# A four-layer graph network on one core: score rows through DRAM in place of transposes, layer 0 divided as it leaves PSUM, and the end graphs' norms in halves

## The chip, the core and the metric

The kernel runs on one core of one Trainium2 chip. Times are device microseconds (us) of one execution. A kernel is run several times and its median is given; one more execution is recorded by the hardware profiler, and everything said of single instructions comes from that one.

## What is computed

The input is 32 graphs of N = 512 nodes with D = 256 features each, and an integer adjacency matrix of 512 x 512 for each graph. Four layers follow one another; each adds its result to its input and normalizes the sum over the features.

```python
# layer 0: four heads of 64, one kind of edge in these data
h = einsum('bnd,hde->bhne', x, W)
weight = leaky_relu(e_src[i] + e_dst[j], 0.01), closed where adj == 0
out = relu(softmax(weight) @ h + bias) + h
x = layernorm(x + (layernorm of out over each head) * gamma + beta)
# layer 1: one head, scores relu(f_src[i] + f_dst[j])
x = layernorm(x + elu(softmax(scores) @ (x @ W)))
# layer 2: a transformer block, 8 heads of 32, edges made symmetric
x1 = layernorm(x + attention(x) @ Wo + bo) * g1 + b1
t  = layernorm(x1 + relu(x1 @ W1 + c1) @ W2 + c2) * g2 + b2      # 256 -> 1024 -> 256
x  = layernorm(x + t)
# layer 3: one head, scores leaky_relu(f_i + f_j, 0.2)
x = layernorm(x + softmax(scores) @ (x @ W))
```

In layers 0, 1 and 3 a score is a function of a sum of one number for the node and one for its neighbour. The kernel takes the exponential of each part once (`ex`), and the unnormalized weight of a pair is the larger of two products of such numbers; so a tile of weights needs one of the parts as a row that lies the same on all 128 partitions (a **score row**, `gb`), and the other as a column.

## The kernel before

**Tiles.** A graph's 512 nodes are R = 4 blocks of 128 partitions; its features lie along the free dimension. All products are in float32. Layers 0, 1 and 3 are products of the 512 x 512 weights (`pt`, four tiles of 128 x 512 per head) with the projected features; layer 2 has scores `s`, their exponentials `pr`, context `cp`, the projection `wop`, and the feed-forward products `f1p` and `f2p`.

**Order.** Each graph is a Python generator that yields before each piece of TensorE work. `heapq.merge` takes the piece with the smallest due place, PERIOD x graph + PLACES[layer][piece] (lines 27 to 46), so that at any time layers 0 and 1 of a later graph, the attention of the one before it and the feed-forward and layer 3 of an earlier one are interleaved. TensorE executes in the order so written. The instructions of VectorE (DVE in the profile), ScalarE (ACT), GpSimd (POOL) and of the transfers (SP) are placed by a scheduler; each of these queues then runs strictly in its order, and an instruction that waits holds back all behind it. `keep_busy` (line 118) puts filler products, 128 x 512 in bf16, ahead of some pieces of the first two and the last two graphs, by the table BUSY (lines 47 to 55). All products have line 112 in the profile and are told apart by their tiles.

**Score rows.** `along` (lines 357 to 367) makes one score row of 512 from a column tile: four TensorE transposes of a column that is broadcast over 128, into one PSUM bank (`gp`), and one ACT copy of 128 x 512 to SBUF (`gb`). Layer 0 has four such rows (one a head), layers 1 and 3 one each. `kept` (line 424, `pt`) is the VectorE instruction that makes a tile of weights from row, column and edges.

**Layer 0** (lines 428 to 515). Products h0p of the inputs; `hv` holds the four heads' values, each with a column of its scale behind it (lines 448 and 453). For each block j, four `pt0`, then eight products `o0` and four `den0` of 32 columns each, four at a time side by side in the array. `den` sums the weights, `o0` holds the unnormalized output, with features on the partitions. Three ACT copies (`back`, L481) take them out of PSUM, twelve transposes (`backp`) turn them back, two reciprocals (L494) of the turned `den` give the divisor, and L501 divides while it applies relu. Then follow x + beta (L509), the addition of h (L510), the norm over each head (lines 306 to 319), gamma (L512), the residual (L513) and the layer's norm.

**Norms.** `layernorm` (lines 284 to 304) takes all four rows at once: four pairs of bn_stats and bn_aggr on VectorE (L290, L291), Ln and Exp on ACT (L282, L283), one small VectorE instruction (L293, `rs`) and four ACT instructions of 128 x 256 (L297), which write the normalized rows.

**Around it.** `transposed` (lines 326 to 338) turns a layer's input: eight transposes (xt1p, xt2p, ytp, xt3p) and two ACT copies (L337). Layer 1 is at lines 532 to 554: h1p, the score row gb1, four `pt1`, the products o1 (in the profile `o<-h,pt`), for each a reciprocal (L547) and two ACT passes (L548, L549), and for each pair of rows two VectorE instructions (L550, L552). In layer 2 the transfers qk (L584) spread the parts of q and k over partitions, L623 to L628 divide by `den`, L653 closes edges and L680 adds up weights. The feed-forward ends with L737 (residual), a norm, L739 and L740 and another norm; layer 3 is at lines 745 to 774, and the finished graph is stored by one transfer (L840). The inputs come by the transfers xt (L779), x (L784), adjt and adj (L372).

Of the kernel before, what the change touches and what calls it, by code (L numbers as in the profile page):

```python
# [28 lines left out]
    "edges": [-3978, -1720, -957, -79],  # L29
    "x": [5375],  # L30
    "mask": [14366, 15324, 18155, 20933],
    "layer 0": [
        -33568, -33515, -33424, -32942, 5301, 7043, 7043, 7043, 8766, 10194, 11091, 11128,
        11993, 11993, 14391,
    ],
    "layer 1": [15460, 15460, 15555, 15555, 15555, 15555, 16382, 17321, 17344, 17344, 17355, 17355],
    "qkv": [18153, 18153, 22255, 22255, 23139, 24065, 25534, 25534, 25534, 25534, 25534],
    "attention": [
        -5960, -4506, -4506, -3927, 26460, 26497, 26497, 26593, 26886, 27435, 27446, 27462,
        28434, 28434, 28779, 29106, 29409, 30200, 31616, 32371, 34290, 34290,  # L40
    ],
    "projection": [34382, 34412, 34412, 34412, 34443],
    "feed forward": [
        36011, 36047, 37566, 38431, 38431, 38519, 38519, 38646, 38646, 38732, 38732, 39499,
        39499, 39646, 39646, 40873, 41200, 41449, 41464,
    ],
    "layer 3": [44919, 44919, 44969, 44969, 44969, 44969, 45682, 48065, 48065, 48065, 48422, 48422],
}
BUSY = {
    ("layer 0", 9): {0: 16, 1: 6},  # L50
    ("layer 1", 1): {0: 72, 1: 40},
    ("layer 1", 8): {0: 4},
    ("layer 3", 1): {-2: 42, -1: 45},
# [27 lines left out]
def fast_path(ctx: ExitStack, tc: tile.TileContext, a: dict, out: bass.AP, bad: bass.AP):  # L81
# [8 lines left out]
    nc = tc.nc  # L90
# [12 lines left out]
    ND = R * (H + 2)  # L103
    NL = 6
    NV = R * (NL + H) + 2 * K
# [157 lines left out]
    ps = ctx.enter_context(tc.tile_pool(name="ps", bufs=2, space=bass.MemoryType.PSUM))  # L263
    stage = ["a"]
# [13 lines left out]
    def all_rows(v):  # L278
        return v.unsqueeze(1).to_broadcast([P, R, D])
# [5 lines left out]
    def layernorm(y, e, mv):  # L285

        st = buf([P, R, 6], "bn", "bn", 2)
        rs = buf([P, 2, R], "rs", "rs", 2)
        for r in range(R):
            nc.vector.bn_stats(st[:, r, :], y[:, r, :])  # L290
            nc.vector.bn_aggr(mv[:, r, :], st[:, r, :])  # L291
        inverse_root(rs[:, 0, :], mv[:, :, 1], e)
        nc.vector.scalar_tensor_tensor(  # L293
            rs[:, 1, :], mv[:, :, 0], -1.0, rs[:, 0, :], op0=ALU.mult, op1=ALU.mult
        )
        for r in range(R):
            nc.scalar.activation(  # L297
                y[:, r, :],
                y[:, r, :],
                AF.Identity,  # L300
                bias=rs[:, 1, r : r + 1],
                scale=rs[:, 0, r : r + 1],
            )

    def head_layernorm(y, e, var):

        G = R * H
        yg = y.rearrange("p r (g d) -> p (r g) d", g=H)
        st = buf([P, 2, G], "lnh", "st", 2)
# [3 lines left out]
        for i in range(2):  # L313
            g = slice(i * G // 2, (i + 1) * G // 2)
            sq = part("sq").rearrange("p (g d) -> p g d", d=HO)
            nc.scalar.activation(sq, yg[:, g, :], AF.Square, scale=HO**-0.5)
            nc.vector.tensor_reduce(var[:, g], sq, axis=X, op=ALU.add)
# [39 lines left out]
    def along(cols, name):  # L357

        yield
        p = bank("gp")  # L360
        for r in range(R):
            product(nc.tensor.transpose,
                    p[:, r * P : (r + 1) * P], cols[:, r, :].to_broadcast([P, P]), ident
            )
        g = part(name)
        nc.scalar.copy(g, p)  # L366
        return g
# [60 lines left out]
    def layer0(x, xt, at, rd, mv, var):  # L428
# [25 lines left out]
        gbs = []  # L454
        for hh in range(H):
            gbs.append((yield from along(ex[:, 0, hh, :].unsqueeze(2), "gb0")))
        den, *ops = (bank(name) for name in ("den0", "o0", "o0"))
        for j in range(R):
            pt = [kept("pt0", gbs[hh], at[:, j, :], ex[:, 1, hh, j : j + 1]) for hh in range(H)]
            yield  # L460
            for hh in range(H):
                for e in range(0, HO, DH):
                    product(nc.tensor.matmul,
                        ops[hh // 2][hh % 2 * HO + e : hh % 2 * HO + e + DH, :],
                        hv[:, j, hh, e : e + DH],
                        pt[hh],
                        start=j == 0,
                        stop=j == R - 1,
                    )
            for hh in range(H):  # L470
                product(nc.tensor.matmul,
                    den[hh * DH : (hh + 1) * DH, :],
                    hv[:, j, hh, HC - DH :],
# [3 lines left out]
                )  # L477
        back = []
        for i, o in enumerate((den, *ops)):
            t = part("back")  # L480
            nc.scalar.copy(t, o)  # L481
            back.append(t)
        y = sb.tile([P, R, D], F32, tag="y", name="y0", bufs=3)
        for i in range(1 + H // 2):
# [6 lines left out]
            if i == 0:  # L491
                rdh = rd.rearrange("p (i r h) -> p i r h", i=H // 2, r=R)
                for i in range(H // 2):
                    nc.vector.reciprocal(  # L494
                        rdh[:, i],
                        p.rearrange("p (r h e) -> p r h e", r=R, h=H)[
                            :, :, 2 * i : 2 * i + 2, DH - 1
                        ],
                    )
                continue  # L500
# [1010 lines left out]
```

## Time and profile before

| | |
|---|---|
| runs | 3490.72, 3491.74, 3490.98 us; median 3490.98 |
| profiled execution | 3491.36 us, of which the span from first to last instruction is 3489.5 |
| mean granted TensorE clock | 0.996 of full |
| instructions | 51983, of these 18579 products and transposes on TensorE |
| HBM | 106.57 MB read, 16.78 MB written; DMA engines busy 32% of the span |

TensorE's queue runs nearly without a gap. The slices of the profile (fortieths of the span) tell where it does not: in the first two and the last one. The first graphs and the last ones have no neighbours to fill the waits of their chains. Between them the picture repeats with every graph. A line of a timeline gives start, length, engine, line, operation, output and inputs, the tile's size and how many instructions it joins; in brackets stands how long the engine had been idle and what ended that. A group of the profile gives total busy time, the mean length of one in ns, and the idle time before. Lengths of TensorE's instructions overlap; the distance of two starts tells what one costs in the queue.

### The profile page before, as it was taken

To read this page: it belongs to the slowest core of one execution; us is meant where nothing else is said; L and a number is where in the kernel's file an instruction comes from. 1 tells how busy PE (TensorE), PEld (TensorE's weight loads), DVE (VectorE), ACT (ScalarE), POOL (GpSimd) and SP (SyncE) were. 2 spreads that over 40 slices of the span, in tenths; PEclk is the share of its full clock that TensorE was granted. 3 is DMA by queue.
4 is the path that set the end of the run, shared out by engine and by line. 5 is a ranking of instruction groups with operands and counts; after the bars stand their busy time and mean duration, and the time that the engine had idled before them with its cause. 6 is when DMAs were issued, how large, how long until landed. Compare 5 with 4: busy or idle time off the path is not lost.

```text
span 3489.5 us, 51983 instructions
## 1 busy us (share of the span) xinstructions
PE 3436.7 (98%) x18579; PEld 2383.9 (68%) x18579; DVE 2889.2 (83%) x5178; ACT 2222.6 (64%) x5729; POOL 81.7 (2%) x171
## 2 busy tenths in 40 slices
PE   7899999999999999999999999999999999999997
PEld 4466767776767776767776767776767776767765
DVE  5778888888888888888888889888889888889863
ACT  3556667666667666667666667666667666666653
POOL 0000000000000000000000000000000000000000
PEclk9999999999999999999999999999999999999999
DMA  4434232334232333232333232334232333232220
GB/s 132 85 76 91 61 85 59 81 79 91 61 85 59 81 79 91 61 85 60 80 79 91 62 84 61 79 79 91 62 84 61 79 79 91 63 84 55 54 55 13
DMA packets 164040, 261.04 MB, mean 75 GB/s; under 512 B 20416, under 2 KB 56384, under 8 KB 163776
## 3 DMA queue, kind: packets, MB, share of 16 engines
q1 hardware_dynamic: 163776, 257.65, 32.0%
q8 instruction: 150, 2.46, 0.3%
q14 instruction: 114, 0.93, 0.1%
HBM read 106.57 MB, written 16.78 MB: 35 GB/s over the span
## 4 chain that ended last, share of the span: by engine, by line
PE 94%; DVE 3%; ACT 1%; issue 1%; DMA 1%; SPq 0%; POOL 0%; ACTq 0%; DVEq 0%; POOLq 0%
PE o L112 20%; PE f2p L112 13%; PE f1p L112 13%; PE s L112 8%; PE qkp L112 6%; PE cp L112 6%; PE den L112 5%; PE h3p L112 3%; PE h1p L112 3%; PE wop L112 3%; PE vp L112 3%; PE h0p L112 3%; PE gp L112 2%; PE backp L112 1%; PE xt3p L112 1%
## 5 line engine op out<-in xcount | busy, mean ns | idle before, releaser
L653 DVE TENSOR_TENSOR pr<-pr,a 128x1024 f32<-128x1024 f32 x384 | 455.5, 1221 | 184.8 <-ACT pr L650 184.8
L424 DVE SCALAR_TENSOR_TENSOR pt<-gb,ex,at 128x512 f32<-128x512 f32 x768 | 538.2, 746 | 33.5 <-ACT gb L366 25.8
L650 ACT ACTIVATE pr<-s 128x512 f32<-128x512 f32 x1024 | 545.3, 617 | 3.0 <-PE s L112 3.0
L112 PE MATMUL f2p<-wf,ft 128*128 128x256 f32 x2048 | 484.8, 380 | 5.5 <-ACT ft L723 5.2
L112 PE MATMUL f1p<-yt,wf 128*128 128x256 f32 x2048 | 483.9, 379 | 0.0
L112 PE MATMUL o<-h,pt 128*128 128x257 f32 x2048 | 475.3, 382 | 2.7 <-DVE pt L424 2.7
L112 PEld LDWEIGHTS o<-h,pt 128*128 128x128 f32 x2048 | 385.6, 190 | 97.5 <-issue 41.8
L680 DVE TENSOR_TENSOR pr<-pr 128x1024 f32<-128x1024 f32 x384 | 447.3, 1213 | 2.8 <-PE cp L112 2.8
L112 PEld LDWEIGHTS f2p<-wf,ft 128*128 128x128 f32 x2048 | 384.0, 190 | 62.9 <-ACT ft L723 9.8
L112 PEld LDWEIGHTS f1p<-yt,wf 128*128 128x128 f32 x2048 | 389.1, 190 | 54.4 <-DVE lo L577 0.5
L297 ACT ACTIVATE y<-y,rs 128x256 f32<-128x256 f32 x768 | 398.1, 593 | 17.0 <-DVE rs L293 17.0
L112 PE MATMUL s<-qk 128*128 128x512 f32 x1024 | 376.5, 469 | 4.6 <-DMA qk<-lo 3.7
L723 ACT ACTIVATE ft<-f1p,cols 128x256 f32<-128x256 f32 x512 | 217.0, 469 | 236.1 <-PE f1p L112 235.3
L290 DVE BATCH_NORM_STATS2 bn<-y 128x6 f32<-128x256 f32 x768 | 300.0, 413 | 5.6
L112 PE MATMUL o<-pt,hv 128*32 128x512 f32 x2048 | 285.0, 602 | 4.7 <-DVE pt L424 4.7
L282 ACT ACTIVATE rs<-mvs,eps1e-05_70 128x4 f32<-128x4 f32 x192 | 57.6, 300 | 325.6 <-DVE mvs L291 321.7
L112 PE MATMUL qkp<-xt,wqkv 128*128 128x512 f32 x512 | 240.5, 603 | 0.0
L112 PE MATMUL cp<-pr,v 128*32 128x512 f32 x2048 | 234.2, 595 | 1.4 <-DVE pr L653 1.4
L112 PEld LDWEIGHTS s<-qk 128*128 128x128 f32 x1024 | 189.0, 192 | 55.5 <-issue 27.6
L112 PEld LDWEIGHTS o<-pt,hv 128*32 128x32 f32 x2048 | 72.7, 109 | 176.5 <-issue 87.4
L576 ACT ACTIVATE hi<-qkp,cols 128x512 fp32r<-128x512 f32 x128 | 88.4, 691 | 164.1 <-PE qkp L112 164.1
L769 DVE RECIPROCAL rd<-o 128x1 f32<-128x1 f32 x128 | 21.6, 168 | 177.5 <-PE o L112 177.3
(140 smaller groups left out, 4949.6 us busy)
## 6 DMA issues: line engine op xcount, KB each, us to landing
qk<-hi SPq DMA_DIRECT2D x512, 128.0 KB, 3.4
qk<-lo SPq DMA_DIRECT2D x512, 128.0 KB, 3.5
adjt<-in_adjt SPq DMA_DIRECT2D x64, 512.0 KB, 3.9
adj<-in_adj SPq DMA_DIRECT2D x64, 512.0 KB, 4.8
xt<-in_xt SPq DMA_DIRECT2D x32, 512.0 KB, 3.8
x<-in_x SPq DMA_DIRECT2D x32, 512.0 KB, 5.2
out<-y SPq DMA_DIRECT2D x32, 512.0 KB, 4.6
wf<-in_w1t SPq DMA_DIRECT2D x1, 1024.0 KB, 9.1
```

Source lines behind the costliest of these rows:

```text
L112: latest[0] = what(*args, **kwargs).ins.name
L282: nc.scalar.activation(out, variance, AF.Ln, bias=eps[e])
L290: nc.vector.bn_stats(st[:, r, :], y[:, r, :])
L297: nc.scalar.activation(y[:, r, :], y[:, r, :], AF.Identity, bias=rs[:, 1, r : r + 1], scale=rs[:, 0, r : r + 1],)
L424: nc.vector.scalar_tensor_tensor(t, g, f, edges, op0=ALU.max, op1=ALU.mult)
L576: nc.scalar.activation(hi, p, AF.Identity, bias=bias)
L650: nc.scalar.activation(t[:, i, :], s, AF.Exp, scale=QSCALE)
L653: nc.vector.tensor_mul(t, t, edges)
L680: nc.vector.tensor_add(t, t, u)
L723: nc.scalar.activation(ft[:, f, :], p[:, f, :], AF.Relu, bias=bf1[:, ff + f : ff + f + 1])
L769: nc.vector.reciprocal(rd[:, r : r + 1], p[:, D : D + 1])
```

## The change

For graphs 1 to 30, called the inner ones, `along` now gives all rows of a layer by one transpose of the columns (16 for layer 0, 4 for layers 1 and 3), one ACT copy of that many partitions by 128, one transfer (a write) into a tile in DRAM, and one transfer (a read) for each row of 512, which reads it from DRAM to all 128 partitions. The first and the last graph, the end graphs, make their rows as before.

In layer 0, `den` is no longer turned back. Its stationary operand is now the scale column broadcast to 32, so that its bank holds the divisor on the same partitions as the outputs; the order of the output's partitions is changed to fit. ACT takes the logarithm of `den` and the exponential of its negative (`inv`), with two sums for the range check; VectorE multiplies the two output banks by `inv` as they leave PSUM; eight transposes follow, and the last step takes relu and adds h in one instruction. The piece count of layer 0 goes from 15 to 11.

In the end graphs the norms of layers 0, 1, 3 and of the feed-forward go in halves of two blocks, and the output is stored in halves. The tiles that hold the values for the range check change size, one of them gets a fourth buffer. The table of due places is new in all layers, and the fillers are fewer: 186 instead of 237 are executed (the new entry for piece 13 of layer 0 is never reached, since the layer has 11). TensorE has 17770 instructions instead of 18579: 630 fewer gp transposes, 128 fewer backp, 51 fewer fillers.

The tables of due places are left out below, as are the lines that pass the graph's number on.

```diff
 BUSY = {
-    ("layer 0", 9): {0: 16, 1: 6},
-    ("layer 1", 1): {0: 72, 1: 40},
+    ("layer 0", 9): {0: 12, 1: 6},
+    ("layer 0", 13): {0: 10},
+    ("layer 1", 1): {0: 48, 1: 34},
     ("layer 1", 8): {0: 4},
-    ("layer 3", 1): {-2: 42, -1: 45},
+    ("layer 3", 1): {-2: 40, -1: 30},
     ("projection", 1): {-1: 8},
     ("layer 3", 8): {-1: 4},
 }
...
-    ND = R * (H + 2)
+    ND = R * 2
...
+    def spans(b):
+        n = R // 2 if b in (0, B - 1) else R
+        return [slice(r, r + n) for r in range(0, R, n)]
...
+    def layernorm(y, e, mv, rows):
+
+        for span in rows:
+            st = buf([P, R, 6], "bn", "bn", 2)
+            rs = buf([P, 2, R], "rs", "rs", 2)
+            for r in range(span.start, span.stop):
+                nc.vector.bn_stats(st[:, r, :], y[:, r, :])
+                nc.vector.bn_aggr(mv[:, r, :], st[:, r, :])
+            inverse_root(rs[:, 0, span], mv[:, span, 1], e)
+            nc.vector.scalar_tensor_tensor(
+                rs[:, 1, span], mv[:, span, 0], -1.0, rs[:, 0, span], op0=ALU.mult, op1=ALU.mult
+            )
+            for r in range(span.start, span.stop):
+                nc.scalar.activation(
+                    y[:, r, :],
+                    y[:, r, :],
+                    AF.Identity,
+                    bias=rs[:, 1, r : r + 1],
+                    scale=rs[:, 0, r : r + 1],
+                )
...
-    def along(cols, name):
+    def along(b, cols, name):
 
         yield
+        n = cols.shape[1]
+        gs = []
+        if b in (0, B - 1):
+            for i in range(0, n, R):
+                p = bank("gp")
+                for r in range(R):
+                    product(nc.tensor.transpose,
+                        p[:, r * P : (r + 1) * P],
+                        cols[:, i + r : i + r + 1].to_broadcast([P, P]),
+                        ident,
+                    )
+                g = part(name)
+                nc.scalar.copy(g, p)
+                gs.append(g)
+            return gs
         p = bank("gp")
-        for r in range(R):
-            product(nc.tensor.transpose,
-                    p[:, r * P : (r + 1) * P], cols[:, r, :].to_broadcast([P, P]), ident
-            )
-        g = part(name)
-        nc.scalar.copy(g, p)
-        return g
+        product(nc.tensor.transpose, p[:n, :P], cols, ident)
+        t = sb.tile([n, P], F32, tag="row", name="row", bufs=2)
+        nc.scalar.copy(t, p[:n, :P])
+        d = dr.tile([n, P], F32, tag=name, name="rows", bufs=2)
+        nc.sync.dma_start(d, t)
+        for i in range(0, n, R):
+            g = part(name)
+            src = d[i : i + R, :]
+            nc.sync.dma_start(g, bass.AP(tensor=src.tensor, offset=src.offset, ap=[[0, P], [1, N]]))
+            gs.append(g)
+        return gs
...
-        gbs = []
-        for hh in range(H):
-            gbs.append((yield from along(ex[:, 0, hh, :].unsqueeze(2), "gb0")))
+        gbs = yield from along(b, ex[:, 0].rearrange("p h r -> p (h r)"), "gb0")
         den, *ops = (bank(name) for name in ("den0", "o0", "o0"))
         for j in range(R):
             pt = [kept("pt0", gbs[hh], at[:, j, :], ex[:, 1, hh, j : j + 1]) for hh in range(H)]
             yield
-            for hh in range(H):
-                for e in range(0, HO, DH):
+            for e in range(0, HO, DH):
+                for hh in range(H):
                     product(nc.tensor.matmul,
-                        ops[hh // 2][hh % 2 * HO + e : hh % 2 * HO + e + DH, :],
+                        ops[e // DH][hh * DH : (hh + 1) * DH, :],
                         hv[:, j, hh, e : e + DH],
                         pt[hh],
                         start=j == 0,
@@ -470,48 +493,48 @@
             for hh in range(H):
                 product(nc.tensor.matmul,
                     den[hh * DH : (hh + 1) * DH, :],
-                    hv[:, j, hh, HC - DH :],
+                    hv[:, j, hh, HO:].to_broadcast([P, DH]),
                     pt[hh],
                     start=j == 0,
                     stop=j == R - 1,
                 )
+        inv = part("inv")
+        nc.scalar.activation(inv, den, AF.Ln)
+        nc.scalar.activation(inv, inv, AF.Exp, scale=-1.0, accum_out=spread0[:, 1:2])
         back = []
-        for i, o in enumerate((den, *ops)):
+        for o in ops:
             t = part("back")
-            nc.scalar.copy(t, o)
+            nc.vector.tensor_mul(t, o, inv)
             back.append(t)
+        nc.scalar.activation(inv, den, AF.Copy, accum_out=spread0[:, 0:1])
         y = sb.tile([P, R, D], F32, tag="y", name="y0", bufs=3)
-        for i in range(1 + H // 2):
+
+        def halves(t, i):
+            return t.rearrange("p r (h i e) -> p r h i e", h=H, i=2)[:, :, :, i]
+
+        for i in range(2):
             yield
             p = bank("backp")
             for r in range(R):
                 product(nc.tensor.transpose,
                     p[:, r * P : (r + 1) * P], back[i][:, r * P : (r + 1) * P], ident
                 )
-            if i == 0:
-                rdh = rd.rearrange("p (i r h) -> p i r h", i=H // 2, r=R)
-                for i in range(H // 2):
-                    nc.vector.reciprocal(
-                        rdh[:, i],
-                        p.rearrange("p (r h e) -> p r h e", r=R, h=H)[
-                            :, :, 2 * i : 2 * i + 2, DH - 1
-                        ],
-                    )
-                continue
             nc.vector.scalar_tensor_tensor(
-                y[:, :, (i - 1) * P : i * P].rearrange("p r (h e) -> p r h e", h=2),
-                p.rearrange("p (r h e) -> p r h e", r=R, h=2),
+                halves(y, i),
+                p.rearrange("p (r h e) -> p r h e", r=R, h=H),
                 0.0,
-                rdh[:, i - 1].unsqueeze(3).to_broadcast([P, R, 2, HO]),
+                halves(h, i),
                 op0=ALU.max,
-                op1=ALU.mult,
+                op1=ALU.add,
             )
         nc.vector.tensor_add(x, x, all_rows(bet0))
-        nc.vector.tensor_add(y, y, h)
-        head_layernorm(y, 1e-6, var)
-        nc.vector.tensor_mul(y, y, all_rows(gam0))
-        nc.vector.tensor_add(y, y, x)
-        layernorm(y, 1e-5, mv[0])
+        for span in spans(b):
+            n = span.stop - span.start
+            ys = y[:, span, :]
+            head_layernorm(y, 1e-6, var, span)
+            nc.vector.tensor_mul(ys, ys, all_rows(gam0, n))
+            nc.vector.tensor_add(ys, ys, x[:, span, :])
+            layernorm(y, 1e-5, mv[0], [span])
...
-        gb = yield from along(ex[:, 0], "gb1")
+        (gb,) = yield from along(b, ex[:, 0, :, 0], "gb1")
         pt = [kept("pt1", gb, at[:, j, :], ex[:, 1, j, :]) for j in range(R)]
...
-        layernorm(y, 1e-5, mv[3])
-        nc.vector.tensor_mul(y, y, all_rows(ln2g))
-        nc.vector.tensor_add(y, y, x)
-        layernorm(y, 1e-5, mv[4])
+            for span in spans(b):
+                if span.stop != r + 2:
+                    continue
+                ys = y[:, span, :]
+                layernorm(y, 1e-5, mv[3], [span])
+                nc.vector.tensor_mul(ys, ys, all_rows(ln2g, span.stop - span.start))
+                nc.vector.tensor_add(ys, ys, x[:, span, :])
+                layernorm(y, 1e-5, mv[4], [span])
...
-        layernorm(x, 1e-5, mv[5])
-        return x
-
-    ends = [0, R * H, R * (H + 1), ND]
+            for span in spans(b):
+                if span.stop == r + 1:
+                    layernorm(x, 1e-5, mv[5], [span])
+                    rows = out[b].rearrange("(r p) d -> p r d", p=P)
+                    nc.sync.dma_start(rows[:, span, :], x[:, span, :])
...
-        mvs = sb.tile([P, 2 * NL * R + H * R + 2 * K], F32, tag="mvs", name="mvs", bufs=3)
+        mvs = sb.tile([P, 2 * NL * R + H * R + 2 * K + 2], F32, tag="mvs", name="mvs", bufs=4)
```

## What the change will do to the time: a prediction

> **What bounds the kernel.** I read the busy shares and the chain of waits first, then the groups of the lines that change, then the timelines of one inner graph.
>
> ```profile
> PE 3436.7 (98%) x18579; PEld 2383.9 (68%) x18579; DVE 2889.2 (83%) x5178; ACT 2222.6 (64%) x5729; POOL 81.7 (2%) x171
> PE 94%; DVE 3%; ACT 1%; issue 1%; DMA 1%; SPq 0%; POOL 0%; ACTq 0%; DVEq 0%; POOLq 0%
> L112 PE MATMUL gp<-ident,ex 128*128 128x128 f32 x768 | 111.4, 277 | 1.5 <-ACT hv L445 0.8 <-ACT ex L536 0.7
> L112 PE MATMUL backp<-ident,back 128*128 128x128 f32 x384 | 52.5, 273 | 1.4 <-ACT back L481 1.4
> L366 ACT COPY gb<-gp 128x512 f32<-128x512 f32 x192 | 108.4, 585 | 0.7 <-PE gp L112 0.6
> ```
>
> TensorE is busy 98% of the span and 94% of the chain: what leaves its queue leaves the time, unless a new wait takes its place. The TensorE timeline of one period:
>
> ```profile
> 1749.62 1.04 PE L112 MATMUL xt2p<-ident,y 128*128 128x128 f32 x8
> ...
> 1836.05 3.72 PE L112 MATMUL h0p<-w,xt 128*128 128x264 f32 x16
> ...
> 1842.53 3.64 PE L112 MATMUL cp<-pr,v 128*32 128x512 f32 x32
> 1846.10 1.09 PE L112 MATMUL xt3p<-ident,y 128*128 128x128 f32 x8
> 1847.12 2.31 PE L112 MATMUL o<-pt,hv 128*32 128x512 f32 x14
> ...
> 1850.65 3.75 PE L112 MATMUL h3p<-w3g,xt 128*128 128x258 f32 x16
> 1854.25 1.03 PE L112 MATMUL xt2p<-ident,y 128*128 128x128 f32 x8
> ```
>
> Columns: start, length, line, product, count. Two xt2p groups are one graph apart: 1854.25 - 1749.62 = 104.63 us. The first xt2p of graph 2 is at 284.78, of graph 30 at 3214.36: 28 periods in 2929.58. The span is thus head 284.8 + 28 x 104.63 + tail 275.1 = 3489.5; the execution took 3491.36, 1.9 more, against a median of 3490.98. I sum against 3491.4.
>
> **Saving in TensorE's order, per inner graph.** Eight transposes in a row take 0.87 us from start to next start (1749.62 to 1750.49), 0.109 each; the 277 ns of the group is a length that overlaps. `along` goes from 24 transposes to 3, layer 0's way back from 12 to 8: 25 x 0.109 = 2.73. Changes between full-width products and 32-column ones (den, o0, cp) cost 0.09 more each by start differences, and the new order has 14 runs of a mode a graph for 12: +0.19. Net **-2.54 us**, 2.4% of a period. (Summing the new order pair by pair, with each pair's start difference in this trace, gives 102.3 us, so -2.3; I keep the count.) The end graphs keep their 24.
>
> **ACT and VectorE, inner graphs.** Layer 0 loses three ACT copies of 0.59 (L481), two small reciprocals and a 1024-wide add (1.14 from start to start); it gains two VectorE multiplies of 512 (0.58 to 0.69 by the rows of L501 and L552) and three ACT passes of 512 (0.60 to 0.64, rows of L623 to L625). Six gb copies of 0.59 become three of 128 columns, about 0.3 (between 0.18 for four columns and 0.40 for 256). ACT gains some 2.5 us a graph, VectorE is about even. Neither is the bound (64%, 83%): nothing, except through the chain below. A fourth mvs buffer and the check tiles: nothing.
>
> **The new wait.** A score row that came by four transposes and one copy now comes by a transpose, a copy, a 2 KB write to DRAM and a 256 KB broadcast read. The read waits for the write on SP, and all later transfers stand behind it there. No row shows this pair. The nearest:
>
> ```profile
> qk<-hi SPq DMA_DIRECT2D x512, 128.0 KB, 3.4
> adjt<-in_adjt SPq DMA_DIRECT2D x64, 512.0 KB, 3.9
> out<-y SPq DMA_DIRECT2D x32, 512.0 KB, 4.6
> a<-in_a SPq DMA_DIRECT2D x3, 256.0 KB, 3.9
> cols<-in_cols SPq DMA_DIRECT2D x1, 9.0 KB, 4.1
> ```
>
> These are medians; the shortest are 2.6 for 128 KB and 3.6 for 512 KB. A line through the shortest gives 2.3 for the write and 2.9 for the read, 5.2 together; through the medians 3.2 + 3.6 = 6.8; the a and cols rows, both from the crowded head, 4.1 + 3.9 = 8.0. Below, the written 2 KB might cost nearly nothing beyond the read: 2.9. I take 5.5, nearest the shortest, as the steady DMA share is 0.33.
>
> Who waits? Layer 0's four reads land 6 to 8 us after their transpose, but VectorE comes to the first pt0 only then (hv add, hv mul, layer 1's work ahead): hidden. Layer 3 has 11 us from gp to o3: hidden. The q and k transfers behind layer 3's read start some 1.3 us late and are wanted 5 us later: hidden. **Layer 1 is tight.** With time 0 at a graph's xt2p, the new order has layer 1's gp at 78.6, o1 at 87.0 to 94.0, cp to 97.8, xt3p at 97.8, h3p directly behind it. gb1 lands near 85.0 (copy and issue 0.9, trip 5.5). Everything behind the first pt1 on VectorE waits: four pt1 at 0.66, the previous graph's FF tail (mul, add, two norms), layer 1's reciprocals and adds. The rs that frees ACT's norm rows, which xt3p reads, is in that queue. In the trace of before it took 11.5 us from f2p's end:
>
> ```profile
> 1830.11 0.69 DVE L737 TENSOR_TENSOR y<-f2p,y 128x512 f32<-128x512 f32 x1 [1.47 <-PE f2p L112]
> ...
> 1841.57 0.28 DVE L293 SCALAR_TENSOR_TENSOR rs<-mvs,rs 128x4 f32<-128x4 f32 x1
> ```
>
> and xt3p began 4.5 us after it. In the new order the last f2p ends at 82.4; with pt1's four (2.6), the two multiplies of hv (2.3) and one pr add (1.1) put between, adding up VectorE's new queue by the cadences of these timelines gives rs at 97.1 and ACT's four rows (2.07, split by pr) done by 98.8: **xt3p waits 1.0**. Then h3p needs ACT's two xt3 copies (0.5 each); before, 3.5 us of layer 0's o and den stood between xt3p and h3p, now nothing does: **0.5 more**. Layer 1's own norm then has 8.3 us from o1's end to xt2p, where it had 18: just enough. So w = 1.5 a graph, following gb1's landing almost one to one: 0.3 if the pair takes 4, 2.8 for 6.8, 4.0 for 8.0.
>
> **A cost that waits can add.** Late in the trace xt3p does wait:
>
> ```profile
> 3306.83 0.33 PE L112 MATMUL xt3p<-ident,y 128*128 128x128 f32 x1 [1.37 <-ACT y L297]
> ...
> 3309.32 5.12 PE L112 MATMUL h3p<-w3g,xt 128*128 128x258 f32 x16
> ```
>
> and the same 16 h3p that took 3.75 above take 5.12; the granted clock of the stretch 3309 to 3316 is 0.78, 3.41 us of it at half rate. [...]
>
> [...]
>
> **Steady sum:** 28 x (-2.54 + 1.5) = **-29 us**.
>
> **Ends.** Head: TensorE's products up to graph 2's xt2p sum to 230.5 us of the 284.8 in the old order and 213.8 in the new (34 fillers at 0.23 gone, gp of graphs 1 and 2, the re-planned order). Fillers cover waits, so I let three of those 16.7 come back as idle time: **-14** (-22 to -6). Tail: products 244.4 to 243.3. Norms in halves let the first two rows go on after half of 1.7 (four bn_stats and aggr) and 2.07 (four ACT rows): 1.9 for each of FF's two, less the extra small instructions of 0.2 to 0.3; the last norm and the 512 KB store (4.6, 128 KB is 3.4) in halves 1 to 1.5: **-5** (-8 to -2).
>
> Sum: -29 - 14 - 5 = -48: **3443 us**, 1.4% less. With w from 0.8 to 2.2 and the ends' bounds: 3412 to 3474.
>
> **Rivals.**
> - *No wait:* the pair takes about 4 us or VectorE's queue is shorter than I add. w = 0.3: 28 x -2.24 = -63, -19: 3409. For it: the chain of before kept 2.3 us to spare. Against: 6 us between gb1's gp and pt1 against 1.1 now.
> - *The row comes late, the saving is eaten:* trip near 6.8, w = 2.8: 28 x 0.26 = +7, -19: 3479. For: the medians of steady transfers. Against: SP is nearly empty around it.
> - *Slower than before:* gb1's pair takes 7.5 or more (write at cols' 4.1, or behind adjt and x on the queues), w = 3.5 or more before xt3p, and half-rate windows follow in half of the periods: 28 x (0.96 + 0.85) = +51, -19: 3523. It decides from w = 2.54 + 19/28 = 3.2. For: the a and cols rows, and the 3306.83 case. Against: those rows are the head's.
> - *The transposes were hidden anyway:* TensorE has no idle time in a period for them (104.63 busy of 104.63 in the windows view); I give it nothing.
>
> **Chances.** Forecast 0.50, no wait 0.19, eaten 0.16, slower 0.15. "Eaten" spreads over 3465 to 3495, a quarter of it within 0.2% (about what a measurement can tell from no change, 7 us). Faster 0.50 + 0.19 + 0.12 = 0.81, same 0.04, slower 0.15. The range 3403 to 3505 leaves out a third of "no wait" and most of "slower": 0.19.
>
> **What would show it.** Right: gp 138 instructions instead of 768, 256 back transposes; xt2p to xt2p about 103.6; before xt3p an idle 1 us released by ACT's norm row L297; DVE idle before the first pt1, released by the gb1 read; landing of the 256 KB reads about 3 us. Wrong if: the gb1 read lands under 4 or over 7 us after its gp, the wait stands elsewhere (o0, s behind SP's queue), the clock falls below 0.98 in steady windows, or the head loses nothing.

## The result: 0.6% slower

The changed kernel takes 3512.92 us (3512.44 to 3513.32, three runs) against 3490.98: 1.0062 times the kernel before, 95% interval 1.0045 to 1.0078. The forecast was 3443 and the range 3403 to 3505; the sign was wrong. Of the 70 us between forecast and result, 43 lie in the periods, 19 in the head and 7 in the tail.

The profiled execution has a span of 3510.7 us, 21.2 more than before. By the first xt2p of graphs 2 and 30 it splits as the prediction split the old one:

| us | before | after | forecast |
|---|---|---|---|
| head | 284.8 | 289.4 | -14 |
| one period, mean of 28 | 104.63 | 105.13 | -1.04 |
| 28 periods | 2929.6 | 2943.8 | -29 |
| tail | 275.1 | 277.5 | -5 |

The busy line from the page of after, and from its view of groups the two kinds of transposes that the change was to save (L110 is now the line of all products):

```profile
PE 3400.4 (97%) x17706; PEld 2282.2 (65%) x17770; DVE 2853.8 (81%) x5174; ACT 2181.4 (62%) x5731; POOL 90.3 (3%) x171
L110 PE MATMUL gp<-ident,ex 128*16 128x128 f32 (+2 forms) x138 | 31.1, 273 | 1.0 <-ACT ex L559 0.7 <-ACT h L789 0.3
L110 PE MATMUL backp<-ident,back 128*128 128x128 f32 x256 | 38.6, 274 | 2.6 <-DVE back L507 2.6
```

The work did go: gp is down from 111.4 to 31.1 us, backp from 52.5 to 38.6, and TensorE is busy 36 us less. Its idle time rose by more. (The chain of waits of this page sums to 12% of the span only, so it is not read.) The windows view of 2500 steady us gives TensorE 2500.00 busy before and 2467.48 after; the waits view of the same stretch, empty before, names three places in 24 graphs:

```profile
PE s L110 <- ACT v L623: 17.6, 20, 1.7
PE xt3p L110 <- ACT y L301: 7.5, 46, 0.2
PE h3p L110 <- ACT xt L343: 5.5, 23, 0.2
```

Columns: waiting group, releaser, us in total, times, longest. The view lists idle time alone; a wait can be shorter there than in the queue: two of xt3p's transposes in one period start 0.49 us apart (1546.92 and 1547.41), where eight in a row take 0.109 each, and the view has 0.16 of this. So I took the distances from start to next start, summed by tile over the 28 periods (us a graph, after less before). A product that starts late thus counts with the tile ahead of it in the queue:

| gp | backp | o0, den0 | s | xt3p | den of layer 2 | h1p | xt2p | o1, o3 |
|---|---|---|---|---|---|---|---|---|
| -2.35 | -0.44 | -0.45 | +0.95 | +1.28 | +0.81 | +0.28 | +0.21 | +0.19 |

The rest is within 0.1 each; the sum is +0.51. What left is what was forecast; xt3p is the wait that was forecast (0.95 of its 1.28 lie between its eight transposes, 0.33 before the h3p behind them); s and den were not.

**The wait at s, followed back** (graph 14's period, which begins at 1552.06). TensorE, then ACT, then VectorE:

```profile
1592.40 1.81 PE L110 MATMUL s<-qk 128*128 128x512 f32 x5 [1.06 <-ACT v L623]
```

```profile
1588.68 0.30 ACT L285 ACTIVATE rs<-mvs,eps1e-05_70 128x4 f32<-128x4 f32 x1 [2.76 <-DVE mvs L295]
1589.01 0.21 ACT L286 ACTIVATE rs<-rs 128x4 f32<-128x4 f32 x1
1589.45 2.08 ACT L301 ACTIVATE y<-y,rs 128x256 f32<-128x256 f32 x4 [0.23 <-DVE rs L297]
1591.43 0.66 ACT L599 ACTIVATE hi<-qkp,cols 128x512 fp32r<-128x512 f32 x1
1592.00 1.17 ACT L623 COPY v<-vp 128x256 f32<-128x256 f32 x4
```

```profile
1575.57 1.29 DVE L430 TENSOR_TENSOR a<-at,adj 128x512 uint8<-128x512 uint8 x2 [1.36 <-DMA adj<-in_adj]
...
1582.39 0.69 DVE L430 TENSOR_TENSOR a<-at,adj 128x512 uint8<-128x512 uint8 x1 [2.05 <-DMA adj<-in_adj]
```

The fourth s waits for a PSUM bank that ACT's copies of v set free. ACT is late with them because layer 3's norm rows stand in front in its queue, and these wait for VectorE's statistics. VectorE is late because it stood still twice, 3.4 us together, for this graph's edges (2.9 in the mean of 24 graphs). They share one buffer with the transposed edges. The new places put the next graph's transposed half (-6702, it was -3978) ahead of them; that half is read at 17.5 us into the period, so the loads are issued at 18.7 and 24.8 and land 4.8 and 5.5 us later. Before, they were issued 36 and 16 us ahead of use and VectorE waited for none; the second of these loads and its first use, in the trace of before:

```profile
1736.45 0.37 SPq L372 DMA_DIRECT2D adj<-in_adj  x1
1752.38 0.68 DVE L405 TENSOR_TENSOR a<-at,adj 128x512 uint8<-128x512 uint8 x1
```

Nothing of this is in the score rows or the division.

### The profile page after: what moved, and what is told of

It is laid out like the page before. It is cut to its first block, busy times and chain, and to the rows that moved or that the text cites. A ratio compares the mean times of both kernels' runs of the same rounds, so it can differ in the third digit from the quotient of the medians.

```text
span 3510.7 us, 50810 instructions
## 1 busy us (share of the span) xinstructions
PE 3400.4 (97%) x17706; PEld 2282.2 (65%) x17770; DVE 2853.8 (81%) x5174; ACT 2181.4 (62%) x5731; POOL 90.3 (3%) x171
## 3 DMA queue, kind: packets, MB, share of 16 engines
HBM read 153.76 MB, written 17.15 MB: 49 GB/s over the span
## 5 line engine op out<-in xcount | busy, mean ns | idle before, releaser
L673 ACT ACTIVATE pr<-s 128x512 f32<-128x512 f32 x1024 | 530.5, 621 | 11.5 <-PE s L110 11.5
L110 PE MATMUL f2p<-wf,ft 128*128 128x256 f32 x2048 | 491.1, 383 | 8.0 <-ACT ft L746 6.0
L110 PE MATMUL f1p<-yt,wf 128*128 128x256 f32 x2048 | 484.2, 379 | 0.6 <-ACT yt L343 0.6
L110 PE MATMUL o<-h,pt 128*128 128x257 f32 x2048 | 469.9, 381 | 0.8 <-DVE pt L449 0.7
L110 PEld LDWEIGHTS f2p<-wf,ft 128*128 128x128 f32 x2048 | 382.1, 190 | 109.3 <-ACT ex L560 25.2
L110 PEld LDWEIGHTS o<-h,pt 128*128 128x128 f32 x2048 | 382.6, 190 | 94.7 <-issue 32.8
L110 PEld LDWEIGHTS f1p<-yt,wf 128*128 128x128 f32 x2048 | 388.4, 190 | 55.6 <-ACT yt L343 1.3
L110 PE MATMUL s<-qk 128*128 128x512 f32 x1024 | 375.5, 470 | 25.9 <-ACT v L623 19.9
L110 PE MATMUL o<-pt,hv 128*32 128x512 f32 x2048 | 274.7, 610 | 5.2 <-DVE pt L449 5.2
L110 PE MATMUL qkp<-xt,wqkv 128*128 128x512 f32 x512 | 246.4, 605 | 0.0
L110 PEld LDWEIGHTS s<-qk 128*128 128x128 f32 x1024 | 188.7, 192 | 78.0 <-ACT v L623 32.5
L110 PE MATMUL cp<-pr,v 128*32 128x512 f32 x2048 | 234.0, 595 | 0.6 <-DVE pr L676 0.6
L285 ACT ACTIVATE rs<-mvs,eps1e-05_70 128x4 f32<-128x4 f32 (+1 forms) x204 | 60.2, 295 | 223.2 <-DVE mvs L295 212.0
L651 DVE TENSOR_TENSOR ct<-ct,dens 128x512 f32<-128x512 f32 x64 | 44.3, 692 | 169.7 <-ACT dens L648 169.7
L110 PEld LDWEIGHTS o<-pt,hv 128*32 128x32 f32 x2048 | 66.5, 110 | 160.9 <-issue 115.8
```

The source lines that it names most:

```text
L110: latest[0] = what(*args, **kwargs).ins.name
L285: nc.scalar.activation(out, variance, AF.Ln, bias=eps[e])
L651: nc.vector.tensor_mul(ct[:, c, :], ct[:, c, :], t)
L673: nc.scalar.activation(t[:, i, :], s, AF.Exp, scale=QSCALE)
```

## The experiments

Each run was timed in three rounds beside the kernel before; "ratio" is to that, with the 95% interval.

### The parts in the old order, and one place in the new

rows_only is the kernel before with `along` as in the change, and div_only the kernel before with layer 0 as in the change but its four gp kept; of layer 0's places those of the pieces that are gone are dropped:

```diff
 rows_only
-        -33568, -33515, -33424, -32942, 5301, 7043, 7043, 7043, 8766, 10194, 11091, 11128,
+        -33568, -33515, -33424, -32942, 5301, 8766, 10194, 11091, 11128,
 div_only
-        11993, 11993, 14391,
+        11993, 14391,
```

oldplan is the changed kernel with the tables PLACES and BUSY of before, both of these lines applied. edge is the changed kernel with one place as before:

```diff
-    "edges": [-6702, -1719, -1658, 725],
+    "edges": [-3978, -1719, -1658, 725],
```

> The kernel before, in its own order of due places, with one thing of the change: the inner graphs' score rows by one transpose and the way through DRAM. Theory 1 (the way through DRAM is cheap, the loss comes from the new order): TensorE loses 21 transposes a graph, 2.3 us; the spare time of 2.3 us before xt3p covers what the rows come later, so a period is 102.3 to 103.0 us and the time 3425 to 3448. Theory 2 (the added transfers crowd SP's queue and the DMA engines, so that q, k and edges land late): new waits before s or pt eat the saving, a period is 104.5 or more and the time 3485 to 3520.

> The kernel before, in its own order, with only layer 0's division as it leaves PSUM (8 transposes back instead of 12, no reciprocals, no separate addition of h); rows by transposes, norms whole. Theory 1: 4 transposes and a little of the changes of mode go, 0.4 to 0.9 us a graph, nothing waits: 3463 to 3480. Theory 3 (the division loads VectorE or delays ACT at a place where TensorE waits): no gain or a loss, 3488 to 3510.

> All of the changed code, in the order (due places) and with the fillers of the kernel before. Theory 1 (the loss is the new order's): the edges' tiles are loaded well ahead again, the wait of 1.3 us before s goes, and a period is 101.3 to 103 us: 3395 to 3445. Theory 2 (the transfers' crowding): a period of 104.5 or more, 3485 to 3520, as the transfers are the same.

> The changed kernel with one due place as before: the load of the next graph's transposed edges at -3978 instead of -6702, which puts it behind the two loads of this graph's own edges in the one buffer they share. Theory 1: VectorE no longer waits for these loads in front of layer 3's norm, so ACT's copies of v, and with them the scores s, come in time: the wait of 1.3 us a graph goes, 3465 to 3490 (the wait of 1.4 at xt3p stays). Theory 2: this place does not matter, 3508 to 3516.

| run | time | ratio | period |
|---|---|---|---|
| rows_only | 3640.5 | 1.0437 (1.0419 to 1.0455) | 109.4 |
| div_only | 3532.7 | 1.0122 (1.0105 to 1.0139) | 105.8 |
| oldplan | 3713.2 | 1.0634 (1.0616 to 1.0652) | 112.0 |
| edge | 3555.7 | 1.0188 (1.0171 to 1.0205) | 106.9 |

Theory 1 fell as it was put: old order with new code is worse than either kernel. All four runs came out above every range that had been set for them, div_only by the least, 23 us. Each shows its own wait.

*rows_only*, waits of TensorE in the same 2500 us:

```profile
PE o L112 <- DVE pt L444: 104.3, 46, 4.1
```

In the old order only 4.9 us lie between layer 1's gp and o1 (8.2 in the new one). The first pt1 comes 5.5 us after gp, 1.4 before. By start distances o1 comes 2.6 us a graph later; layer 0's first o0, which stands behind xt3p in this order, 2.8, and its other o0 1.4; of the 104.3 us of that line 38.4 lie at o1 and 66.0 at layer 0's o0. The granted clock falls to 0.979 from 0.996. Here the way through DRAM is late, as in the prediction's slower rival, but at the first users of the rows and not at xt3p. *oldplan* has the same wait (109.4 us in that view) beside div_only's loss: 104.6 + 4.7 + 1.2 = 110.5 of its 112.0.

*div_only* follows theory 3, and loses more than that gave it. It has no wait in that view, and 0.44 us less backp, but o0 and den0 take 1.7 more. At two of the four blocks VectorE delivers the tiles pt0 just in time; from the end of the last tile to the next product after den0 it is 1.89 us before and 2.75 here. In the old layout the last head's two outputs lie in two groups of 32 columns; in the new one its two outputs and its den all lie in one. The 0.86 is measured at both blocks; that the shared group is its cause is my reading of the layout and was not shown. The starts fit it: at the end of such a block in div_only the last products begin singly, 0.43 us apart, in before in pairs, 0.20 apart.

*edge* fits neither theory's range. It does what was said of s (its distances fall by 1.0 us), but the scheduler, which finds the edges in SBUF sooner, moves the maxima (L430) from 23 and 30 us into the period to 99, 103 and 6, where VectorE had no gap. New waits at den of layer 2, o0 and den0 cost 2.8 net.

### Taking the edges' loads away, and VectorE's load

adj_late is the changed kernel with two buffers for the edges (one in place of two for norm statistics, divisor and row), the loads left in their old place, and the maxima of `symmetric` written inside the loop over the q and k products; adj_late2 has `(1, 1)` in the second line:

```diff
-        t = sb.tile([P, R // 2, N], I32, tag="adj", name=name, bufs=1)
+        t = sb.tile([P, R // 2, N], I32, tag="adj", name=name, bufs=2)
...
                 yield
+                if (c, s) == (1, 0):
+                    a2 = symmetric(at, ts)
                 p = bank("qkp")
```

no_bias (after) and no_bias_b (before) leave out the addition of layer 0's bias; rows_t is the changed kernel with transposes for all graphs:

```diff
 no_bias, no_bias_b
-        nc.vector.tensor_add(values, h, bias0)
-        nc.vector.tensor_mul(values, values, scale)
+        nc.vector.tensor_mul(values, h, scale)
 rows_t
-        if b in (0, B - 1):
+        if True:
```

(Views and broadcasts are left out of the three lines of no_bias.)

> The changed kernel with the edges' loads taken off VectorE's way: a second buffer for them (for SBUF's sake norm statistics, one divisor tile and the row tile keep one buffer instead of two), so that both halves are loaded early, and the two maxima written between the q and k products, about 17 us into a period, where they stand now, not earlier. Theory 1 (the wait of 1.3 us before s comes from these loads, through layer 3's norm and ACT's copies of v): it goes and no other takes its place, 103.6 to 104.3 us a period, 3465 to 3495. Theory 4 (VectorE has no idle time from 83 us of a period to 15 us of the next, and that stretch sets the period, whatever waits are taken away outside of it): 104.8 us or more, 3500 to 3530.

> The changed kernel without the addition of layer 0's bias to the values (one VectorE instruction of 128 x 1024, 1.14 us, about 90 us into a period); the bias is left out of the result. Theory 4: it stands in the stretch where VectorE is full and TensorE waits at xt3p, so the period shortens by 0.9 to 1.4 us: 3470 to 3490. Theory 2 (transfers crowd each other): no change, 3505 to 3520.

> The kernel before with the same instruction left out. Its TensorE waits for nothing in a period, so all theories expect at most the ends to move: 3478 to 3491. A gain of 20 or more would say that VectorE bounded the kernel before as well.

> The changed kernel, its order and fillers kept, with the score rows of all graphs by transposes and copies again. TensorE gets 2.3 us a graph back, ACT some 2.6. Theory 1 and 4 (the way through DRAM is hidden in this order): the wait at xt3p shrinks by what TensorE is later, but ACT is later too; 105.5 to 107.5 us a period, 3520 to 3580. Theory 2 (the transfers are what costs): the period falls below 104.8, 3450 to 3500.

> As the run with two buffers for the edges, with the two maxima written one piece later, between the last two q and k products, some 33 us into a period, where VectorE has idle time, and behind layer 0's and layer 3's tiles of weights instead of among them. Theory 1 (price of the edges' loads 1.3 us a graph): no wait at s, and layer 0's products of block 3 no longer late: 103.5 to 104.2 us a period, 3465 to 3490. Theory 4 (the full stretch sets the period): as the maxima now stand outside it, also some 104; it forecasts that the wait of 1.4 at xt3p stays, as nothing was taken from the stretch.

| run | time | ratio | period |
|---|---|---|---|
| adj_late | 3504.0 | 1.0042 (1.0028 to 1.0056) | 104.9 |
| adj_late2 | 3467.7 | 0.9937 (0.9920 to 0.9953) | 103.74 |
| no_bias | 3580.8 | 1.0253 (1.0233 to 1.0273) | 107.8 |
| no_bias_b | 3482.0 | 0.9974 (0.9962 to 0.9985) | 104.35 |
| rows_t | 3540.6 | 1.0143 (1.0126 to 1.0160) | 106.6 |

*adj_late* ends the wait at s (-1.35 us) with the maxima still ahead of layer 3's norm; what went is VectorE's wait for the edges, 68.6 us in 24 graphs before this edit (first line) and 12.4 with it:

```profile
DVE a L430 <- DMA adj<-in_adj: 68.6, 48, 2.6
DVE a L437 <- DMA adj<-in_adj: 12.4, 22, 1.3
```

But its maxima stand before block 3's tiles, and o0 and den0 there pay 1.13; so its time lies in theory 4's range, though the wait went as theory 1 had it. *adj_late2*, one piece later, pays nothing: s falls by 1.36, no other tile by more than 0.03. It beats both kernels, and its waits are the forecast ones alone:

```profile
PE xt3p L110 <- ACT y L301: 7.9, 48, 0.2
PE h3p L110 <- ACT xt L343: 5.7, 24, 0.2
```

So the wait at s is the edges' loads, and its price is 105.13 - 103.74 = 1.39 us a graph, 39 of the 45 us between the two kernels.

*no_bias* took 1.1 us off VectorE and lost 68 us. The scheduler orders VectorE's and ACT's queues anew for each program; here it set three additions of weights ahead of layer 1's last rows. VectorE of no_bias, then of after, at the same place:

```profile
1572.86 3.46 DVE L700 TENSOR_TENSOR pr<-pr 128x1024 f32<-128x1024 f32 x3
1576.24 0.68 DVE L570 SCALAR_TENSOR_TENSOR relu<-exp,relu 128x512 f32<-128x512 f32 x1
```

```profile
1543.95 1.22 DVE L703 TENSOR_TENSOR pr<-pr 128x1024 f32<-128x1024 f32 x1
1545.09 0.16 DVE L297 SCALAR_TENSOR_TENSOR rs<-mvs,rs 128x4 f32<-128x4 f32 x1
1545.16 0.69 DVE L573 SCALAR_TENSOR_TENSOR relu<-exp,relu 128x512 f32<-128x512 f32 x1
```

The norm that xt2p needs comes that much later (start distances: h3p +1.5, xt2p +1.2). Part of it is the clock, 0.984 in this run. The run tested the order, not the load, and says nothing of theory 4. *rows_t* is 28 us slower than the changed kernel, in the range of theories 1 and 4, but not by the rows alone: VectorE's wait for the edges grows from 2.9 to 5.6 us a graph, and s waits 1.5 by the same chain (0.7 in after). So the rows' worth is not read from it but from late2_t below, where that wait is gone.

### Fillers and halves

fill is the changed kernel, late2_fill is adj_late2, with these fillers; whole is the changed kernel, late2_tail is adj_late2, with other spans:

```diff
 fill, late2_fill
-    ("layer 0", 9): {0: 12, 1: 6},
+    ("layer 0", 9): {0: 16, 1: 6},
-    ("layer 1", 1): {0: 48, 1: 34},
+    ("layer 1", 1): {0: 72, 1: 40},
-    ("layer 3", 1): {-2: 40, -1: 30},
+    ("layer 3", 1): {-2: 42, -1: 45},
 whole
-        n = R // 2 if b in (0, B - 1) else R
+        n = R
 late2_tail
-        n = R // 2 if b in (0, B - 1) else R
+        n = R // 2 if b == B - 1 else R
```

> The changed kernel with as many filler products as before (237 for 186), its new order kept. [...] Theory 6 (the head's waits are for VectorE and ACT, fillers fall into them anyway): 3511 to 3520, as some fillers stand in nobody's wait.

> The same with the fillers of before. [...] A candidate that could beat both kernels: 3460 to 3490.

> The changed kernel with the end graphs' norms and the last store whole, as before; all else new. If the halves are worth what was forecast (about 3 us in the head, 4 to 5 in the tail), 3519 to 3522; if the first half of a norm only starts the transposes earlier and the next product waits for the second half anyway, 3512 to 3516.

> The faster variant with the norms in halves in the last graph only, whole ones in the first. If the halves are worth some 8 us in the tail and lose 2 in the head, as the run with whole norms has it: 3462 to 3467. If the head's loss there was something else: 3467 to 3472.

Fill: 3510.0 (1.0058; 1.0041 to 1.0075), three below after. late2_fill: 3470.5 (0.9946; 0.9930 to 0.9963), three above adj_late2. The number of fillers decides nothing here. Whole: 3514.4 (1.0070; 1.0053 to 1.0087). Its tail is 285.9 us, 8.4 longer than after's, so the halves earn 8.4 there; its head is 286.9, 2.5 shorter, and its periods 105.0. So its time falls where halves worth nothing had been put, while in the tail they were worth more than forecast. late2_tail: 3468.4 (0.9941; 0.9925 to 0.9958), head 286.9 against adj_late2's 283.2, tail 1.2 shorter: here whole norms cost the head 3.7. The two disagree on the head's sign, and heads of equal design lie between 277 and 291 as the queues are ordered anew. What halves are worth in the head stays open.

### Do the rows through DRAM pay?

late2_t and late2_g1t are adj_late2, rows_g1t is rows_only, with another condition in `along`; late2_pool1 and late2_pool2 are adj_late2 with work moved to GpSimd (views left out again):

```diff
 late2_t
-        if b in (0, B - 1):
+        if True:
 late2_g1t, rows_g1t
-        if b in (0, B - 1):
+        if b in (0, B - 1) or name == "gb1":
 late2_pool1, late2_pool2
-        nc.vector.tensor_add(values, h, bias0)
+        nc.gpsimd.tensor_add(values, h, bias0)
 late2_pool2
-        nc.vector.tensor_mul(values, values, scale)
+        nc.gpsimd.tensor_mul(values, values, scale)
```

> The faster variant (edges in two buffers, maxima 33 us in) with the score rows of all graphs by transposes and copies. If the way through DRAM pays in this order once the edges' loads are out of the way: TensorE gets 2.3 us a graph back, of which the wait of 1.4 at xt3p takes some: 104.6 to 106.2 us a period, 3490 to 3535. If the rows' saving is worth nothing because VectorE's full stretch sets the period: 103.6 to 104.2, 3463 to 3480.

> The faster variant with layer 1's score row alone by transposes, so that nothing waits for its way through DRAM; layers 0 and 3 stay. Theory A (the wait at xt3p is VectorE's queue, which has no idle time there): the wait stays between 1.1 and 1.5, TensorE gets 0.3 us a graph: 3471 to 3482. Theory B (it is the late landing of layer 1's row, as the prediction had it): the wait falls by 0.8 or more, 3440 to 3460.

> The kernel before with the rows of layers 0 and 3 alone through DRAM, layer 1's by transposes. Theory A (in the old order layer 1's row has only 5 us to its first use, and its trip makes o1 and all that VectorE has behind it late): the waits before o1 go and those at xt3p and o0 shrink, 103 to 105.5 us a period, 3440 to 3515. Theory B (layer 0's four rows are late as well, or the transfers crowd each other): 107 us or more, 3565 to 3640.

> The faster variant with the addition of layer 0's bias (128 x 1024, 1.14 us on VectorE, 90 us into a period) on GpSimd, which is idle there; its result is wanted 14 us later. Theory 4 (VectorE's stretch without idle time, from 85 us of a period to 15 of the next, sets the period): the waits at xt3p and den2 shrink by up to 1.1 us together, 102.6 to 103.4 a period, 3435 to 3460. If TensorE waits there for something else: 103.6 to 104.2, 3464 to 3482. GpSimd might be so slow that o0 waits for it: above 3482.

> The same with the multiplication by the scale behind it on GpSimd too: 2.3 us off VectorE's stretch. Theory 4: the waits of 1.4 at xt3p and 0.7 at den2 go, 102.0 to 103.0 a period, 3415 to 3450, unless GpSimd's two instructions together come later than o0.

| run | time | ratio | period |
|---|---|---|---|
| late2_t | 3468.4 | 0.9939 (0.9922 to 0.9955) | 103.97 |
| late2_g1t | 3470.5 | 0.9950 (0.9933 to 0.9966) | 104.00 |
| rows_g1t | 3563.0 | 1.0210 (1.0192 to 1.0227) | 106.7 |
| late2_pool1 | 3611.9 | 1.0347 (1.0330 to 1.0365) | 108.9 |
| late2_pool2 | 3611.1 | 1.0347 (1.0330 to 1.0364) | 108.6 |

*late2_t* is the run that settles the change's main idea. With all rows by transposes TensorE has 2.27 us more of gp in each period, and the period is 0.23 longer. The one wait that its view lists:

```profile
PE h3p L110 <- ACT xt L343: 5.7, 24, 0.2
```

The 2.27 replaces waits: xt3p -0.95, den of layer 2 -0.70, o0 and den0 -0.49. *late2_g1t* gives layer 1's row without a trip, and xt3p waits as before (2.27 us for the group, 2.28 in adj_late2): that wait is not the row's landing. The 0.33 us of transposes that it adds do cost, 0.27 a graph; they stand elsewhere in TensorE's queue than the rest of the 2.27. In after, adj_late2 and late2_t VectorE runs from 86 us of a period to 11 us into the next with 1.0 us of idle time, in late2_g1t with 1.8, in the kernel before with 0.2.

*rows_g1t* takes back 2.7 of the 4.7 us a graph that rows_only lost; its time lies just below theory B's range, yet both theories hold in part. Layer 1's trip is over half of the loss in the old order. The waits at o1 are gone, those at layer 0's o0 are as they were:

```profile
PE o L112 <- DVE pt L444: 66.7, 25, 4.7
```

So layer 0's four rows are late there too: SP issues their reads 3.1 us after the write (median; 1.4 in after), and the first pt0 begins 3.4 us behind the first xt3p, where before it began with it. VectorE waits 0.7 us a graph of this for a read; the rest is its order, as in the example looked at two additions of weights stand ahead of that pt0. Why the reads are issued later there was not followed up.

*late2_pool1* and *2* took 1.1 and 2.3 us off VectorE, and lost 5 a graph: in both, three additions of weights again stand ahead of layer 1's last rows; in the first VectorE waits 2.6 us for GpSimd as well, whose addition takes 2.37. The clock falls to 0.980 and 0.983. That VectorE's load sets the period was thus not shown; that its order can lengthen it was.

## Why the prediction was wrong, point by point

- **The saving in TensorE's order: right.** 2.73 for 25 transposes; measured 2.35 + 0.44.
- **ACT and VectorE "nothing, except through the chain": incomplete.** The division, alone in the old order (div_only), cost 0.86 at each block that waits for its tile; in the new order block 3's last tile ends 2.75 before the next product, against 1.89.
- **The new wait: right in size, wrong in cause.** Forecast 1.0 at xt3p and 0.5 at h3p; measured 0.95 between xt3p's transposes and 0.33 ahead of h3p. But "following gb1's landing almost one to one" is refuted by late2_g1t. By the trace it is VectorE's queue: rs comes 4.5 us ahead of xt3p in the old order and 1.0 in the new. That half of the working held: rs forecast at 97.1, measured at 98.4 behind the wait at s, and at 96.7 in adj_late2 without it.
- **The trip: near.** Forecast 2.3 for the write and 2.9 for the read. The 8 KB write lands in 1.3 (the landing of two is known), the next read issues 1.2 after a 2 KB write, and reads land in 3.7 (median of those known, nearly all layer 0's; the four known of single rows in 3.1): 4.3 to 4.9, for the 5.5 that I took.
- **The step that failed, in the periods: the sum took the new order as given, and added up one chain of it.** I followed the rows, VectorE's queue around xt3p, and SP's queue for q and k. The list under "Who waits?" has the score rows and the q and k transfers; the loads of the edges, which moved as well, stand in no term of the sum, though the change gives their new places. They cost 1.39 us a graph, 39 us. Without them the periods come to 28 x (103.74 - 104.63) = -25, for a forecast of -29. That this is so near is in part luck: den of layer 2, h1p, xt2p and o1, o3 cost 1.5 us a graph that no term had, and o0, den0 and s gave 0.9 back.
- **A further miss, argued in part: which resource sets the period.** "TensorE has no idle time in a period" is true of the kernel before, and I took it for a proof that transposes removed are time removed. In adj_late2 2.27 us of them were worth 0.23: what left the queue came back as waits at xt3p, den and o0. By the releasers in the trace these are waits for VectorE, at first or second hand, which has 1.0 us of idle time in that stretch. That its load is the cause is not shown, since every run that took load off it was ordered anew.
- **Head: -14 became +4.6.** Graph 0's xt2p begins 8.1 us earlier, and it bought nothing:

```profile
87.58 1.09 PE L112 MATMUL xt2p<-ident,y 128*128 128x128 f32 x8
...
91.32 5.42 PE L112 MATMUL qkp<-xt,wqkv 128*128 128x512 f32 x12
```

```profile
79.46 0.33 PE L110 MATMUL xt2p<-ident,y 128*128 128x128 f32 x1 [1.57 <-ACT y L301]
79.95 0.33 PE L110 MATMUL xt2p<-ident,y 128*128 128x128 f32 x1 [0.16 <-ACT y L301]
84.16 1.82 PE L110 MATMUL xt2p<-ident,y 128*128 128x128 f32 x6 [3.88 <-ACT y L301]
...
91.29 1.98 PE L110 MATMUL qkp<-xt,wqkv 128*128 128x512 f32 x4
```

First before, then after: two of the eight transposes start early, the other six at 84.16, and qkp at 91.3 in both. The failed term is the time beyond the products, which I let grow by three of the 16.7 us of products saved: it grew by all of them and 4.6 more. Of these 21.3 us the trace shows 15.6 as more idle time of TensorE (46.3 for 30.7); and the time at half the clock doubles, from 17.1 to 34.1 us (mean granted clock of the head 0.97 and 0.94), for which the sum had nothing. What each is worth was not separated.
- **Tail: -5 became +2.4.** The halves earned 8.4 by the run with whole norms, more than forecast. But without them the new order's tail is 10.8 longer than before's. Some 3.5 of this is a block of 16 o0 and 8 den0 which stood ahead of graph 30's xt2p (3207.24 to 3210.77 in the old trace) and now stands behind it; the rest was not followed up.
- **A cost that waits can add: not paid in the periods.** The granted clock is 1.00 in the steady windows of after (300 to 3200 us), with waits of about 1 us at two places of nearly every period. The 0.85 a period that the slower rival adds is my estimate, half of what the one case's 3.41 us at half rate lose; no run shows that such windows come in every second period, and none came there. In rows_only, with waits of 7 us a graph, the clock is 0.979 over the whole run. How much idle time brings a drop is not shown: in the old trace TensorE is busy 6.96 us of the 7 from 185 to 192 and all of the 8 from 192 to 200, and the clock is 1.00 in the first stretch and 0.57 in the second.

## What to carry to other kernels

When two engines have hardly any idle time in the same stretch, work taken off one of them may come back as a wait for the other, as 2.04 of 2.27 us did here; look for that before adding up what a busy engine loses. In a kernel whose order is re-planned, cost every moved transfer, those of inputs first: which buffer it takes, who used it last, and when that user reads. A variant that takes away one wait is read by where the instructions went, since the scheduler can order its queues anew after a small edit, as in no_bias.

## What the runs showed that I had not expected

Leaving out 1.1 us of VectorE work a graph cost 68 us in one kernel, where the queues came out in another order, and gained 7 in the other, which was not followed up. In the kernel that beats both, the score rows may come by transposes or through DRAM: 3468.4 and 3467.7 us, with 106.57 and 153.76 MB read from HBM, and no difference beyond the spread of the runs. The tie is one of the whole alone: through DRAM the 28 periods are 6.4 us shorter (0.23 each), while the head and the tail are 4.8 longer (283.2 and 278.2, against 279.7 and 277.0), and such ends vary from one ordering to the next.
